# One transfer for each quarter of the routing weights, half of the sorted down matrices kept on chip, and another choice of sorted batches, in a fused mixture-of-experts and attention kernel

## The chip, the cores and the metric

The kernel runs on one core of a Trainium2 chip. The metric is the device time of one execution in microseconds (us). A core has five engines with a queue each, which work in parallel and wait for each other through semaphores: PE (TensorE, matrix products), ACT (ScalarE), DVE (VectorE), POOL (GpSimd) and SP (SyncE). SP computes nothing here: it issues nearly all transfers. A transfer, once issued, is carried by the core's 16 DMA engines. Each queue is strictly in order, so an instruction that waits holds everything behind it.

## The reference

The input is x, 8 batches of 1024 tokens of 128 numbers, all in float32. Three steps follow each other, each added to x:

```
x = x + 0.5 * ffn(layernorm(x))
x = x + causal_attention(layernorm(x))        # one head of 128, rotary positions
x = x + 0.5 * ffn(layernorm(x))               # the same weights again

ffn(h): scores = sigmoid(h @ gate_w.T);  idx = top4(scores + gate_b)
        w = 2.5 * scores[idx] / sum(scores[idx])
        y = sum over 16 experts e of  comb[:, e] * ((silu(h @ gate_e) * (h @ up_e)) @ down_e)
            + the same form with one shared expert, unweighted
```

An expert has 64 inner units; each token uses 4 of the 16 experts.

## The kernel before

**Two ways to compute the ffn.** Tokens are handled in groups of 512 (four tiles of 128), two groups to a batch. Over the two ffn layers there are 32 groups. Twenty are *dense* (class `Group`): all 16 experts are computed for all tokens, two experts (one pair) per step on the 128 partitions, and the product with `comb` zeroes what a token did not choose. Twelve are *sorted* (class `SortedGroup`), in three chunks of two batches (`CHUNKS`: batches 4 and 5 of the first ffn, then 0 and 1, then 2 and 3 of the second). A chunk counts and places its tokens, scatters normalised rows into a DRAM buffer ordered by expert (`scatter`, L1041, indirect transfers from POOL), works through that buffer in ten double blocks of 1024 rows (class `Rows`), writes results to DRAM, and each token gathers its four results back (`gather`, L868, POOL) and adds them (`gathered`, L877, DVE).

**A dense group.** `gate` (L677) and `up` (L683) are 512-wide products per pair; `gate_act` (ACT), `units` (L694, DVE) and `weigh` (L699, DVE, or POOL as a help) make the hidden tile; `down` (L710) sums nine terms per token tile. `weigh` needs the tile `cb`: for each pair, the routing weights of its two experts, spread over 64 partitions each. The weights are turned on PE, stored to a small DRAM tensor `cd` (`store_weights`, L610) and read back with a broadcast over partitions (`load_weights`, L619) in four quarters of two pairs each. The pairs are experts 2n and 2n+1, so each quarter takes two transfers, one per half of the partitions:

```
for h in range(2):
    nc.sync.dma_start(
        out=cb[h * I : (h + 1) * I, :, :],
        in_=self.pairs[h, part * N : (part + 1) * N, :].unsqueeze(0).broadcast_to([I, N, W]),
    )
```

Here I is 64, N is 2 and W is 512. There are `CBP` = 4 quarter tiles in all, so a quarter of the next group can be loaded once both `weigh` of that quarter are done.

**A double block of sorted rows.** `load` (L1112) brings two times 512 rows, `turn` (L1143) transposes them on PE, `up` (L1154) multiplies with a table of gate and up matrices that lies on chip and is addressed by a register, and after the activation and `turn_units`, `down` (L1187) multiplies with the down matrices `wt`, which `load_down` (L1136) fetches from DRAM with eight small transfers of 32 KB, each at an address read from the sorted owners; `wt` has two buffers. Results leave by `store` (L1200).

**The order.** The program is not written in the order in which it is issued. Class `Plan` is a list scheduler at build time: every step has an engine, an estimated duration, a rank (lower first), the steps it follows and the buffers it takes and frees. It writes one fixed order per engine. Rank constants are `UNITS`, `WEIGH`, `ATTEND`, `SORT`, `READY`, `EXPERTS`, `HELP`, from 0 to 5000; `PATIENCE` says how long ACT puts off a step that needs another function table. The framework gives SP's transfers eight completion semaphores in turn, so a transfer waits for the one issued eight before it.

Of the kernel before, what the change touches and what calls it, by code (L numbers as in the profile page):

```python
# [43 lines left out]
class Plan:  # L44
# [6 lines left out]
    PATIENCE = 2.0  # L51
    RATE, LAND = 0.23, 1.9

    def __init__(self, begin):
        self.steps = []
        self.places = {}
        self.lines = {}
        self.held = {}
        self.free_at = dict.fromkeys(self.ENGINES, begin)
        self.transfers = begin  # L60
        self.port = begin
        self.table = None
# [9 lines left out]
    def add(self, engine, work, rank, emit, after=(), take=(), free=(), table=None, moves=0,  # L72
            port=False):
        s = Step(engine, work, rank, emit, take, free, table, moves, port)
        for a in after:
            if a.engine is None:
                s.ready = max(s.ready, a.end)
            else:
                a.next.append(s)
                s.left += 1  # L80
        self.steps.append(s)
        return s
# [58 lines left out]
    def run(self):  # L141
# [12 lines left out]
        while todo:  # L154
# [30 lines left out]
            self.free_at[e] = end = t + work  # L185
            if s.port:
                self.port = end
            if s.moves:
                self.transfers = max(end + 0.5, self.transfers) + s.moves / self.RATE
                end = self.transfers + self.LAND  # L190
# [11 lines left out]
def kernel(  # L202
# [30 lines left out]
    CHUNKS = ((0, (4, 5)), (1, (0, 1)), (1, (2, 3)))  # L233
# [28 lines left out]
    for name, n, shape in (  # L262
        ("x", 9, [P, GT, D]),
        ("xn", 3, [P, GT, D]),
        ("xnc", CB * NG + 1, [P, GT, D]),
        ("hT", 3, [P, W]),
        ("hTs", 2, [P, W]),
        ("hTa", 1, [P, W]),
        ("lt", 2, [P, P]),
        ("sc", 3, [P, GT, E]),  # L270
        ("bi", 3, [P, GT, E + TOPK]),
        ("m8", 3, [P, GT, 8]),
        ("rp", 3, [P, GT, E + TOPK]),
        ("sel", 3, [P, GT, E]),
        ("comb", 3, [P, E, GT]),
        ("cT", 2, [P, P]),
        ("cb", CBP, [P, NP // CBP, W]),
        ("sg", 4, [P, W]),
        ("sh", 2, [P, W]),
        ("hid", NP + 2, [P, W]),  # L280
        ("q", 1, [P, S]),
        ("k", 1, [P, S]),
        ("v", 1, [P, NT, D]),
        ("pr", 2, [P, S]),
        ("prT", 2, [P, NT, P]),
        ("chosen", 1, [P, CT, E]),
        ("combc", 1, [P, CT, E]),
        ("at", 1, [P, CT, E]),
        ("top", 1, [P, CT, 8]),
        ("eq", 1, [P, GT, TOPK, E]),  # L290
        ("row", 4, [P, GT, D]),
        ("got", 4, [P, TOPK + 1, D]),
        ("wt", 2, [P, GT, D]),
        ("un", 2, [P, W]),
        ("hs", 2, [P, W]),
    ):
        plan.pool(name, n)
        buffers[name] = [sbuf(shape, f"{name}{m}") for m in range(n)]
# [93 lines left out]
    nc.sync.dma_start(out=wd, in_=w_down.rearrange("(n p) d -> p n d", p=P))  # L392
# [6 lines left out]
    table = sbuf([P, E * D], "table")  # L399
    cs = sbuf([P, 2, S], "cs")  # L400
# [105 lines left out]
    class Group:  # L506
# [101 lines left out]
        def store_weights(self):  # L608
# [4 lines left out]
            self.pairs = cd.rearrange("(n h) s -> h n s", h=2)  # L613

        def load_weights(self, part):
            N = NP // CBP
            cb = buf("cb", (self.id, part))
            for h in range(2):
                nc.sync.dma_start(  # L619
                    out=cb[h * I : (h + 1) * I, :, :],  # L620
                    in_=self.pairs[h, part * N : (part + 1) * N, :].unsqueeze(0).broadcast_to([I, N, W]),
                )

        def spread_steps(self, rank, after, shared, turned):
# [9 lines left out]
            for m in range(CBP):  # L634
                loads.append(
                    sp(
                        2.0 / CBP, rank + 0.01 * m, lambda m=m: self.load_weights(m),
# [91 lines left out]
        def expert_steps(self, p, last, hT, turned, weights, shared):  # L729
# [31 lines left out]
            for part, tiles in enumerate(self.parts):  # L761
# [3 lines left out]
                for k, s in enumerate([*ready, shared]):  # L765
                    steps.append(
                        pe(
                            0.89 * share, rank - 0.5 + 0.1 * part,
# [36 lines left out]
    class SortedGroup(Group):  # L805
# [57 lines left out]
        def fetch(self, j):  # L863
            nc.sync.dma_start(out=buf("got", (self.id, j))[:, TOPK, :], in_=self.kept[:, j, :])
# [10 lines left out]
        def gathered(self, j, k):  # L875
            got = buf("got", (self.id, j))
            nc.vector.scalar_tensor_tensor(  # L877
                got[:, TOPK, :], got[:, k, :], self.chunk.weight[:, self.n * GT + j, k : k + 1],
                got[:, TOPK, :], ALU.mult, ALU.add,
            )  # L880

        def store_sorted(self, j):
            t = self.g * GT + j
            to = in_tiles(out, self.b, slice(t, t + 1)) if self.layer else self.kept[:, j : j + 1, :]
            nc.sync.dma_start(out=to, in_=buf("got", (self.id, j))[:, TOPK : TOPK + 1, :])

        def gather_steps(self, rank, after):
            ends = []
            for j in range(GT):
                a = (self.id, j)  # L890
                r = rank + 0.02 * j
                before = [
                    sp(
                        0.5, r, lambda j=j: self.fetch(j), after=[*after, self.away],
                        take=[("got", a, 1)], moves=0.064,
                    )
                ]
                for k in range(TOPK):
                    got = [
                        pool(  # L900
                            1.27, r, lambda j=j, k=k: self.gather(j, k),
                            after=before if k == 0 else [*after, first], moves=0.064,
                        )
                    ]
                    first = got[0] if k == 0 else first
                    before = [
                        dve(
                            0.36, r, lambda j=j, k=k: self.gathered(j, k), after=[*got, *before],
                            port=True,
                        )  # L910
                    ]
                ends.append(
                    sp(
                        0.5, r, lambda j=j: self.store_sorted(j), after=before, free=[("got", a)],
                        moves=0.064,
                    )
                )
            return ends

    class Chunk:  # L920
# [126 lines left out]
        def steps(self, rank, later, begins, cleared):  # L1047
# [52 lines left out]
            for m, gr in enumerate(self.groups):  # L1100
                gr.ends = gr.gather_steps((later if self.layer == 0 else SORT + 1500 + 10 * n) + 3 + m * 0.1, [*done, *w])

    class Rows:
# [22 lines left out]
        def load_down(self):  # L1126
            w = buf("wt", self.id)
            for h in range(2):
                q = 2 * self.i + h
                _, rows = nc.values_load_multi_w_load_instructions(  # L1130
                    self.chunk.owner[0:1, NS + q * GT : NS + (q + 1) * GT],
                    engines=[mybir.EngineType.SP], min_val=0, max_val=(E - 1) * I,
                    skip_runtime_bounds_check_because="the owner is held below the number of experts",
                )
                for j, row in enumerate(rows):
                    nc.sync.dma_start(  # L1136
                        out=w[h * I : (h + 1) * I, j, :], in_=w_down[bass.ds(row, I), :]
                    )
# [44 lines left out]
        def down(self):  # L1183
            for j in range(GT):
                for h in range(2):
# [3 lines left out]
                        buf("wt", self.id)[rows, j, :],  # L1189
# [15 lines left out]
        def steps(self, rank, owner, scattered, in_front):  # L1205
# [3 lines left out]
                moves=0.25,  # L1209
# [286 lines left out]
    def load_table(n):  # L1496
# [5 lines left out]

    have_table = chain(
        sp, READY, [given(100.0)], *[(0.5, lambda n=n: load_table(n)) for n in range(2)], moves=1.0
# [16 lines left out]
    cleared = [given(40.0)]  # L1521
    rows_free = []
    for m in range(2):
        cleared = [
            chain(
                sp, SORT + 900, cleared,
                *[(0.5, lambda m=m, part=part: clear(10 * m + part, 20)) for part in range(10)],
                moves=5.2,
# [129 lines left out]
```

## Time and profile before

| | |
|---|---|
| median of 3 runs | 925.82 us (921.67 to 927.11) |
| the profiled execution: its own time | 927.32 us |
| its span, first to last instruction | 925.5 us |
| mean granted TensorE clock | 0.987 |
| PE, DVE, POOL, ACT busy | 882.7, 689.1, 568.5, 555.3 us |
| bytes moved | 139.52 MB in 173694 packets |
| transfers `cb<-cd` | 160 of 256 KB |
| transfers `wt<-in_w_down` | 240 of 32 KB |

Busy time is the union of an engine's instructions. PE's matrix products are pipelined, and a float32 product shows as two instructions. A group's row reads: line, engine, operation, output and inputs by name, count, busy time, mean duration in ns, then the idle time before it and what ended it. "issue" stands for time in which the engine waited for nothing that the profile shows. "SPq" rows are the time in which SP's queue was issuing. The DMA row of the page is the mean busy share of all 16 DMA engines; it doesn't tell one engine from another. In the list of queues, q1 holds what SP issues, q0 the indirect transfers of POOL.

### The profile page before, as it was taken

To read this page: it belongs to the slowest core of one execution; us is meant where nothing else is said; L and a number is where in the kernel's file an instruction comes from. 1 tells how busy PE (TensorE), PEld (TensorE's weight loads), DVE (VectorE), ACT (ScalarE), POOL (GpSimd) and SP (SyncE) were. 2 spreads that over 40 slices of the span, in tenths; PEclk is the share of its full clock that TensorE was granted. 3 is DMA by queue.
4 is the path that set the end of the run, shared out by engine and by line. 5 is a ranking of instruction groups with operands and counts; after the bars stand their busy time and mean duration, and the time that the engine had idled before them with its cause. 6 is when DMAs were issued, how large, how long until landed. Compare 5 with 4: busy or idle time off the path is not lost.

```text
span 925.5 us, 17703 instructions
## 1 busy us (share of the span) xinstructions
PE 882.7 (95%) x5364; PEld 628.9 (68%) x5364; DVE 689.1 (74%) x2194; ACT 555.3 (60%) x1065; POOL 568.5 (61%) x597
## 2 busy tenths in 40 slices
PE   8899999989999999999899999999998989999998
PEld 5547576558587767778677676667576967666665
DVE  5767888848887776877577898687887646687875
ACT  6566644887875566776467567777657535334321
POOL 3442378887446788547475768887865672177560
PEclk9998999999999999999999999999999989999999
DMA  7979661144576844575566543142567567666671
GB/s 218 237 189 246 165 169 37 35 118 127 139 188 173 223 128 125 157 187 141 161 164 153 158 114 116 39 117 68 153 153 191 147 199 202 174 175 170 156 180 35
DMA packets 173694, 139.52 MB, mean 151 GB/s; under 512 B 17760, under 2 KB 144288, under 8 KB 173472
## 3 DMA queue, kind: packets, MB, share of 16 engines
q1 hardware_dynamic: 160032, 111.95, 46.0%
q0 software_dynamic: 12288, 25.19, 9.7%
q10 hardware_dynamic: 1280, 1.26, 0.4%
q8 instruction: 43, 0.70, 0.3%
q14 instruction: 51, 0.42, 0.1%
HBM read 90.49 MB, written 47.84 MB: 149 GB/s over the span
## 4 chain that ended last, share of the span: by engine, by line
PE 58%; POOL 19%; issue 7%; DMA 5%; ACT 4%; DVE 4%; SPq 1%; ACTq 0%; POOLq 0%; DVEq 0%
PE psum L710 13%; POOL rows L1041 12%; PE psum L677 9%; PE psum L683 9%; PE psum L1154 5%; DMA row<-rows 3%; PE psum L1434 3%; PE psum L1143 3%; PE psum L650 3%; PE psum L1187 2%; PE psum L1393 2%; POOL got L868 2%; PE psum L496 2%; PE psum L1421 1%; POOL mv_f L471 1%
## 5 line engine op out<-in xcount | busy, mean ns | idle before, releaser
L868 POOL DMA_INDIRECT got<-results,place x192 | 189.2, 985 | 99.5 <-issue 45.0
L1041 POOL DMA_INDIRECT rows<-xnc,place x192 | 194.8, 1014 | 75.5 <-issue 54.4
L710 PEld LDWEIGHTS psum<-wd,hid 128*128 128x128 f32 x1280 | 159.9, 194 | 33.1 <-issue 20.3
L710 PE MATMUL psum<-wd,hid 128*128 128x128 f32 x1280 | 168.3, 279 | 4.8 <-issue 2.5
L690 ACT ACTIVATE sg<-psum 128x512 f32<-128x512 f32 x160 | 94.5, 597 | 121.6 <-PE psum L677 98.9
L677 PE MATMUL psum<-hT,wg 128*128 128x512 f32 x320 | 164.7, 596 | 1.7 <-ACT sg L690 1.6
L683 PE MATMUL psum<-hT,wu 128*128 128x512 f32 x320 | 163.4, 592 | 0.0
L694 DVE TENSOR_TENSOR hid<-psum,sg 128x512 f32<-128x512 f32 x160 | 109.3, 688 | 56.5 <-PE psum L683 46.9
L683 PEld LDWEIGHTS psum<-hT,wu 128*128 128x128 f32 x320 | 60.8, 190 | 76.5 <-issue 71.5
L699 DVE TENSOR_TENSOR hid<-hid,cb 128x512 f32<-128x512 f32 x132 | 100.7, 770 | 3.0
L1434 PEld LDWEIGHTS psum<-v,prT 128*128 128x128 f32 x576 | 70.1, 192 | 14.3 <-issue 7.8
L1434 PE MATMUL psum<-v,prT 128*128 128x128 f32 x576 | 74.1, 278 | 1.8 <-DVE prT L1425 1.3
L1393 PE MATMUL psum<-k,q 128*128 128x512 f32 (+2 forms) x192 | 71.0, 504 | 3.9 <-POOL k L1310 3.5
L677 PEld LDWEIGHTS psum<-hT,wg 128*128 128x128 f32 x320 | 51.9, 191 | 26.3 <-issue 20.0
L877 DVE SCALAR_TENSOR_TENSOR got<-got,wk 128x128 f32<-128x128 f32 x192 | 65.2, 358 | 3.8 <-DMA got<-results,place 2.1
L1306 POOL TENSOR_TENSOR sg<-sg,cs 128x512 f32<-128x512 f32 x32 | 40.3, 1281 | 44.7 <-ACT sg L1296 44.5
L1154 PE MATMUL psum<-table,hTs 128*128 x480 | 64.3, 282 | 0.1
L1154 PEld LDWEIGHTS psum<-table,hTs 128*128 128x128 f32 x480 | 59.3, 195 | 5.6 <-issue 2.2
L455 DVE BATCH_NORM_STATS2 st<-x 128x6 f32<-128x128 f32 x192 | 53.2, 277 | 11.2 <-DMA x<-in_x 5.1
L1407 ACT ACTIVATE pr<-psum,top 128x128 f32<-128x128 f32 (+3 forms) x64 | 47.5, 745 | 12.1 <-DVE top L1402 11.7
L1425 ACT COPY prT<-psum 128x512 f32<-128x512 f32 (+3 forms) x85 | 37.2, 477 | 27.0 <-PE psum L1421 25.1
L1393 PEld LDWEIGHTS psum<-k,q 128*128 128x128 f32 x192 | 32.8, 196 | 26.3 <-issue 16.1
(148 smaller groups left out, 1515.5 us busy)
## 6 DMA issues: line engine op xcount, KB each, us to landing
cb<-cd SPq DMA_DIRECT2D x160, 256.0 KB
row<-rows SPq DMA_DIRECT2D x60, 256.0 KB
results<-row SPq DMA_DIRECT2D x60, 256.0 KB
rows<-sums SPq DMA_DIRECT2D x20, 512.0 KB
wt<-in_w_down SPq DMA_DIRECT2D x240, 32.0 KB
x<-in_x SPq DMA_DIRECT2D x16, 256.0 KB
kept<-x SPq DMA_DIRECT2D x12, 256.0 KB
rows<-xnc,place POOLq DMA_INDIRECT x192
```

Source lines behind the costliest of these rows:

```text
L677: nc.tensor.matmul(pair_of(("gu", self.id, k))[0], wg[:, k * P : (k + 1) * P], self.hT(), start=True, stop=True,)
L683: nc.tensor.matmul(pair_of(("gu", self.id, k))[1], wu[:, k * P : (k + 1) * P], self.hT(), start=True, stop=True,)
L690: nc.scalar.activation(buf("sg", a), pair_of(a)[0], AF.Silu)
L694: nc.vector.tensor_tensor(buf("hid", a), pair_of(a)[1], buf("sg", a), ALU.mult)
L699: engine.tensor_tensor(hid, hid, cb, ALU.mult)
L710: nc.tensor.matmul(y[:, cols], units[:, cols], wsd if k == NP else wd[:, k, :], start=(self.terms[part] == 1 and j == tiles[0]), stop=(sel ...
L868: nc.gpsimd.indirect_dma_start(out=buf("got", (self.id, j))[:, k, :], out_offset=None, in_=self.chunk.results, in_offset=bass.IndirectOffs ...
L877: nc.vector.scalar_tensor_tensor(got[:, TOPK, :], got[:, k, :], self.chunk.weight[:, self.n * GT + j, k : k + 1], got[:, TOPK, :], ALU.mul ...
L1041: nc.gpsimd.indirect_dma_start(out=row_views[self.n % 2][t * TOPK + k], out_offset=bass.IndirectOffsetOnAxis(ap=self.place[:, t, k : k + 1 ...
L1154: nc.tensor.matmul(p[:, cols], buf("hTs", (self.id, h))[:, cols], table[:, bass.ds(self.at[h][j], D)], start=True, stop=True,)
L1393: nc.tensor.matmul(s[:, c:e], q[:, i * P : self.width], k[:, c:e], start=True, stop=True)
L1434: nc.tensor.matmul(o, buf("prT", self.id)[:, j, :], buf("v", self.b)[:, j, :], start=(j == 0), stop=(j == i),)
```

## The change

- `load_weights`: the pairs are now experts n and n+8 (the gate, up and down matrices are laid out to match by the host and by two loads of `wd`), so that a quarter of the weights of one half is contiguous in DRAM, and one transfer fills all 128 partitions of a quarter. Its step is costed 0.6 instead of 0.5.
- `load_down` fetches only the second half of a double block (four transfers instead of eight). For the first half, `down` reads a tile `low` on chip, loaded once, which holds all 16 down matrices in partitions 0 to 63, at an address in a register; partitions 64 to 127 of `low` are four `wt` buffers.
- `gather_steps`: one fetch and one store per sorted group instead of four of each. The sum is made in a tile of the pool `x` (which has nine), and `got` loses its fifth row.
- `un` and `hs` get one buffer each instead of two.
- `CHUNKS`: batches 5 and 6 are sorted in the first ffn, not 4 and 5.
- The planner: `PATIENCE` 3.5 instead of 2.0; SP's transfers are modelled with eight lanes (`LANES`), several pieces where a step issues several; `down` of a dense group is ranked behind that group's own gates (+0.5 instead of -0.5); the gathers of the second ffn are ranked `SORT + 500` instead of `SORT + 1500`, ahead of `READY`; the clearing of the second row buffer may start at 160 instead of following the first.

```diff
-    PATIENCE = 2.0
+    PATIENCE = 3.5
+    LANES = 8
...
+            if s.moves and e == "SP":
+                end = t
+                for _ in range(s.pieces):
+                    end = max(end, self.lanes[self.lane]) + work / s.pieces
+                    self.transfers = max(end + 0.5, self.transfers) + s.moves / s.pieces / self.RATE
+                    self.lanes[self.lane] = self.transfers + self.LAND
+                    self.lane = (self.lane + 1) % self.LANES
...
-    CHUNKS = ((0, (4, 5)), (1, (0, 1)), (1, (2, 3)))
+    CHUNKS = ((0, (5, 6)), (1, (0, 1)), (1, (2, 3)))
...
-        ("got", 4, [P, TOPK + 1, D]),
-        ("wt", 2, [P, GT, D]),
-        ("un", 2, [P, W]),
-        ("hs", 2, [P, W]),
+        ("got", 4, [P, TOPK, D]),
+        ("un", 1, [P, W]),
+        ("hs", 1, [P, W]),
...
-            self.pairs = cd.rearrange("(n h) s -> h n s", h=2)
+            self.pairs = cd.rearrange("(h n) s -> h (n s)", h=2)
...
-            for h in range(2):
-                nc.sync.dma_start(
-                    out=cb[h * I : (h + 1) * I, :, :],
-                    in_=self.pairs[h, part * N : (part + 1) * N, :].unsqueeze(0).broadcast_to([I, N, W]),
-                )
+            nc.sync.dma_start(
+                out=cb.rearrange("p n s -> p (n s)"),
+                in_=self.pairs[:, part * N * W : (part + 1) * N * W].unsqueeze(1).broadcast_to(
+                    [2, I, N * W]
+                ),
+            )
...
-                            0.89 * share, rank - 0.5 + 0.1 * part,
+                            0.89 * share, rank + 0.5 + 0.1 * part,
...
-        def fetch(self, j):
-            nc.sync.dma_start(out=buf("got", (self.id, j))[:, TOPK, :], in_=self.kept[:, j, :])
+        def fetch(self):
+            nc.sync.dma_start(out=x_of(self.b, self.g), in_=self.kept)
...
-                gr.ends = gr.gather_steps((later if self.layer == 0 else SORT + 1500 + 10 * n) + 3 + m * 0.1, [*done, *w])
+                gr.ends = gr.gather_steps((later if self.layer == 0 else SORT + 500 + 10 * n) + 3 + m * 0.1, [*done, *w])
...
-            for h in range(2):
-                q = 2 * self.i + h
+            q = 2 * self.i + 1
...
+                nc.sync.dma_start(
+                    out=buf("wt", self.id)[I:, j, :], in_=w_down[bass.ds(row, I), :]
+                )
...
-                        buf("wt", self.id)[rows, j, :],
+                        buf("wt", self.id)[rows, j, :] if h else low[rows, bass.ds(self.at[0][j], D)],
```

## The prediction

> **What bounds the kernel now.** I read the page's busy times first, then the rows over time, the queues, PE's waits, and SP's own instructions.
>
> ```profile
> PE 882.7 (95%) x5364; PEld 628.9 (68%) x5364; DVE 689.1 (74%) x2194; ACT 555.3 (60%) x1065; POOL 568.5 (61%) x597
> ...
> PEclk9998999999999999999999999999999989999999
> DMA  7979661144576844575566543142567567666671
> ```
>
> PE is at work in 882.7 of 925.5 us; only 43 us of it are idle. The change neither adds nor drops a matrix product, so a gain can only come out of those 43 us and the few slices in which the granted clock dips. The DMA row has room: its mean over 16 engines is 56.5% (the sum of the shares below). That is what a change that makes transfers worse would eat.
>
> ```profile
> q1 hardware_dynamic: 160032, 111.95, 46.0%
> q0 software_dynamic: 12288, 25.19, 9.7%
> ...
> cb<-cd SPq DMA_DIRECT2D x160, 256.0 KB
> ...
> wt<-in_w_down SPq DMA_DIRECT2D x240, 32.0 KB
> ```
>
> SP's queue q1 carries 112 MB, of which the routing weights (`cb<-cd`) are 42 MB: the largest stream. Next, what PE waits for:
>
> ```profile
> PE psum L1143 <- DMA row<-rows: 10.5, 8, 3.3
> PE psum L1421 <- ACT pr L1407: 4.7, 5, 1.4
> PE psum L496 <- DVE q L1299: 3.5, 2, 3.0
> ```
>
> The largest wait, 10.5 us in 8 pieces, is for blocks of sorted rows. Two slices around such waits also show the clock down:
>
> ```profile
> 450.00:475.00 25.00, 22.29 (x142) 16.21 (x140) 15.61 (x45) 15.50 (x31) 12.45 (x14) 0.93 0.70 189
> ...
> 750.00:775.00 25.00, 21.77 (x133) 17.17 (x134) 11.71 (x36) 11.82 (x23) 16.03 (x17) 0.86 0.73 199
> ...
> 850.00:875.00 25.00, 25.00 (x124) 15.76 (x123) 20.67 (x56) 9.63 (x16) 13.63 (x15) 1.00 0.66 161
> ```
>
> (columns: window, length, busy us and count of PE, PEld, DVE, ACT, POOL, then clock, DMA share, GB/s). Lost clock: (1 - 0.93) and (1 - 0.86) times 25, 1.75 + 3.5 = 5.25 us. In the last row PE is busy throughout: the dense tail. Why rows come late is seen on SP:
>
> ```profile
> L1136 SPq DMA_DIRECT2D wt<-in_w_down x240: 427/469/1696, 133.4 to 786.9; - x120
> ...
> L619 SPq DMA_DIRECT2D cb<-cd x160: 573/605/3438, 25.9 to 899.4; - x160
> ```
>
> (min/median/max ns of one issue, first and last start). The eight `wt` issues of a double block stand in one queue with its row loads; in the timeline one such eight takes 5.5 to 7.0 us.
>
> **The change, part by part.** The sums are made against the profiled execution, 927.3 us (span 925.5 and 1.8 around it), which lies 1.5 above the median of 925.8.
>
> *Half of the down matrices from chip.* 120 issues of 0.54 us (0.469 and two register rows of 37 and 29 ns) leave SP: 65 us by the medians, and 80 to 105 by the 5.5 to 7.0 us of an eight. They are not on PE's path themselves; what they release is the row loads behind them. Of the 10.5 us I take 9 as gone and of the 5.25 us of clock 4. The loads of `low` (0.5 MB, once, near 100 us) lie beside other work. PE gets 120 more products with a register address: the chain of waits shows eight such pairs (L1154 x16) at 1.78 to 1.98 us, against 1.79 for L710 x16, so 0 to 0.02 us each, 0 to 2.8 us; I take 1, because most of these pieces show 1.79.
>
> *One fetch and one store per sorted group, one `un` and `hs`.* SP loses 72 issues of 0.43 to 0.50 us. The sum moves into an `x` tile, which four groups of the first chunk hold at once; the loads of other batches stand behind these fetches in SP's queue. Cost on PE's path between -1 (reloads wait less) and +5 (one late batch, like the 5.7 us wait for `row<-rows` in the chain); I take 0. With single `un` and `hs`, a wait of `turn_units` would have the other double block's products queued behind it; the order puts those between, so 0, and up to 0.8 us per block if not (the largest wait of L1178).
>
> *Batches 5 and 6 first.* Batch 4's attention no longer waits for gathered rows: the L1421 wait of 1.1 us at 521 us goes, and something like it may return one batch later. I take -1.5, with bounds -2 and 0.
>
> *Order.* `down` behind the gates, gathers ranked ahead, `PATIENCE`: ACT has 90 table loads in both orders, and the first 60 us of PE's order are almost the same. The clearing of the second buffer moves behind 160 us; where it was (75 to 100, DMA share 1.04) PE was 24.95 of 25 us busy, so nothing is to be won. Two of SP's queue positions matter: the weights of the second group still stand behind ten clearing transfers.
>
> So far -9 - 4 - 1.5 + 1 = -13.5 us.
>
> *One transfer for a quarter: the part that decides.* By the issue row alone it is a gain: 80 issues of 0.605 us fewer, 48 us of SP. But compare how the source is walked. Before, its outermost dimension is the broadcast over I = 64 partitions, `[64, 2, 512]`, and so is the target's. Now the source is `[2, 64, 1024]`: outermost 2, the two halves; the target has 128. No transfer of the trace of before has an outermost dimension under 64, so no row here prices that. The Trainium skill does. In "DMA: Bandwidth & Descriptors", section "Why a DMA increments its semaphore by 16 and not by 1", it says that the number of DMA engines a transfer runs on is the largest up to 16 that divides the outermost dimension (not 1) of *both* sides. Before: 64 and 64, so 16 engines. Now: 2 and 128, so **two engines**, and always the lowest ones. The same page's "Rules for kernel authors" pulls the other way: it tells one to replace two transfers to disjoint partition halves by one over 128 partitions, since both share the same engines. The change follows the second rule and runs into the first.
>
> The price by the row (16 engines): the trace's packet records show the 2 KB packets of q1 at 126 ns mean; 160 x 128 / 16 x 0.126 = 161 us per engine over the whole run, much of it hidden, and the sum stays at -13.5. By the rule: a quarter is 128 packets of 4 KB, 64 on each of two engines. A 4 KB packet is between the 2 KB ones (86 ns at the quiet start, 121 median later) and the 8 KB ones of the rope load (314): 162 to 185 ns by straight lines; POOL's own 4 KB packets show 187 median, 224 mean. I take 175. A quarter then takes 64 x 0.175 = 11.2 us, a group 45, all twenty 80 x 11.2 = 896 us, on those two engines. They also carry their sixteenth of everything else: 0.460 x 925.5 - 161 + 0.097 x 925.5 + 7 (the small queues) - 14 (half of `wt`, 7680 packets of 30 ns) = 348 us. Together 1244 us: **the two engines become the bound**. To that, the start before the first weights (25.9 us, some 17 of them already used by other loads) adds 9, and the end, the last quarter's `weigh`, `down` and store, 10: 1263. What hides part of it now, the room in the DMA row, does not help, since it is on the other fourteen. The -13.5 us of PE lie beside it and count nothing. Check by pace: the dense tail runs a group in 23 us (513 PE instructions in the four windows from 800 to 900, about 120 per group); at 45 us and more its five groups alone add 110 us. Every row load that SP issues after a quarter has its share in the same two rings and lands 11 us later per quarter in front of it. I take **1260 us**; its own range is 1150 (162 ns, packed without gaps, and 20 less of other traffic) to 1480 (224 ns gives 1147 + 348; rows late).
>
> **The rivals.**
> *A, two engines (forecast), 1260.* For: the outermost sizes, which can be read in the code, and a rule stated for exactly them. Against: no row here shows it.
> *B, sixteen engines all the same: faster, 912.* If the rule doesn't hold for such a source, what remains is a relieved SP: 927.3 - 13.5 = 913.8 in the profile, 912 as a median. For: the 10.5 us of row waits and the two clock dips sit where SP issues without pause. It decides as soon as a quarter lands in 3 us or so.
> *C, sixteen engines, but gates first starve on DVE: 938.* With `down` behind, eight gate pairs run back to back at 1.72 us (L1286 x4 in the chain), while DVE needs 0.688 + 0.770, and 0.358 for a gathered row, 1.82 us: 0.8 us per group, and about 1.3 when a routing chain falls in. 20 x 1.3 = 26 us, 913.8 + 26 - 1.5 = 938. From 0.7 us per group it eats the gain, from 1.2 it makes the kernel over 1% slower. Against: DVE is only 74% busy and three pairs are in flight.
>
> **How the numbers follow.** A 0.72, B 0.20, C 0.08. About 1% is what a measurement of this kernel tells from no change. Faster: B, less the 0.03 in which its gain stays under 9 us, 0.17. Within 1%: those 0.03 and half of C, 0.07. Slower: A and the other half of C, 0.76. The predicted time is that of A. As A leaves out more than 2 in 10, the range reaches over C to B: 905 to 1450, leaving some of each end out.
>
> **What would show it.** A: the page lists `cb<-cd` x80 at 512 KB; PE falls to about 70% busy, with its clock often down; the mean DMA share *falls* to about 37% (2 x 896 + 16 x 348 engine-us over 16 x 1260), though transfers hold everything up; the largest waits are `hid` at `weigh` (L720) for `cb<-cd`, and `row<-rows`. B: PE above 96%, the L1159 wait for rows under 3 us, no clock dip after 450. C: waits of `wg`/`wu` products for `hid`/`sg` at the top of PE's list. The forecast is wrong if a quarter lands within about 5 us of its issue; the size is wrong if a 4 KB packet takes far from 175 ns.

## The result and the profile after

The changed kernel takes **1303.99 us** (median of 4 runs, 1300.91 to 1304.76) where the kernel before takes 926.19 (921.67 to 927.11) on the same chip: a ratio of **1.409** (95% interval 1.4035 to 1.4138). The forecast was 1260. The profiled execution took 1300.91 us by itself, its span is 1299.1, and the mean granted TensorE clock is 0.865.

First the page of the changed kernel: busy times, the rows of the clock and of the DMA engines, the two large queues, the shares of the chain that ended last, and the transfers of the routing weights.

```profile
PE 962.3 (74%) x5364; PEld 685.6 (53%) x5364; DVE 683.1 (53%) x2187; ACT 561.0 (43%) x1072; POOL 562.8 (43%) x597
...
PEclk9798879996878879978898898999798777978876
DMA  6251142521211144433453443212335343522211
...
q1 hardware_dynamic: 131552, 108.52, 26.1%
q0 software_dynamic: 12288, 25.19, 7.0%
...
DMA cb<-cd 33%; DMA row<-rows 13%; PE psum L731 5%; DMA results<-row 4%; PE psum L698 4%; PE psum L704 3%; DMA kept<-x 3%; PE psum L1170 3%; DMA cd<-cT 2%; PE psum L1159 2%; PE psum L1409 2%; POOL rows L1059 2%; DMA x<-kept 2%; PE psum L1450 2%; SPq L638 1%
...
cb<-cd SPq DMA_DIRECT2D x80, 512.0 KB
```

PE is at work for 74% of the span and its clock dips everywhere, not in two slices. The DMA row has *fallen*: 26.1 + 7.0 + 0.7 for the small queues is 33.8%, against 56.5% before. Read alone, it says that transfers have room. The line of the chain says the opposite: a third of the chain is the landing of `cb<-cd`. Both are true if a few of the sixteen engines carry that stream, so that the mean over sixteen hides how full those few are. The 80 transfers of 512 KB show that the change did what it says.

The list of waits (us in total, times, longest):

```profile
DVE hid L720 <- DMA cb<-cd: 184.7, 28, 11.1
...
PE psum L1159 <- DMA row<-rows: 129.6, 14, 22.1
...
POOL hid L720 <- DMA cb<-cd: 102.5, 11, 28.7
```

`weigh` (L720) waits 287 us for routing weights on DVE and POOL together. In the kernel before the one such wait of note was a single one of POOL's:

```profile
POOL hid L699 <- DMA cb<-cd: 15.8, 1, 15.8
```

The wait of the row transposes went from 10.5 to 129.6 us. The chain in order of time (start, length, what) shows the weights at the start and at the end:

```profile
28.71 40.60 DMA cb<-cd
...
82.92 20.21 DMA cb<-cd
103.12 23.74 DMA cd<-cT
127.57 18.26 DMA cb<-cd
...
1148.22 87.08 DMA cb<-cd x3
1237.01 19.67 DMA cb<-cd
1257.79 29.55 DMA cb<-cd
```

The first group's weights take 40.6 us; a dense group of the old tail took 23 us in all. By the packet records its four quarters land one after the other, at 38.6, 48.6, 58.8 and 68.8 us. At 103 us even the small store of a group's weights (`cd<-cT`, 32 KB) needs 23.7 us, and only then can the group's own quarters start: the packet records show an earlier group's quarters under way through all of that time, from 86 to 126 us. The tail is the weights and little else: the last quarter lands at 1287.3. By stage (window, length, busy us and count of PE, PEld, DVE, ACT, POOL, clock, DMA share, GB/s):

```profile
1200.00:1299.00 99.00, 62.19 (x234) 43.00 (x234) 35.24 (x73) 10.14 (x17) 17.12 (x18) 0.76 0.20 71
```

The row of the old tail showed PE busy in 25.00 of 25 us, at clock 1.00 and a DMA share of 0.66. Here it is busy in 62 of 99, at 0.76, with a DMA share of 0.20. Last, SP's own instructions (ns of one issue: min/median/max):

```profile
L638 SPq DMA_DIRECT2D cb<-cd x80: 484/632/18359, 26.5 to 1257.8; - x80
```

The median issue is about what it was (605), and there are half as many. But one of them now holds SP for 18 us, where the longest of them before was 3.4, and it is not alone: 33 of SP's 432 issues take over 8 us, and all of them together 850 us, against 396 for the 702 issues of the kernel before. What such an issue waits for is not shown.

The packet records of the trace (start, duration, bytes and queue of each packet, but not its engine) settle the size. SP's 10240 packets of 4 KB, all of them routing weights, take 159 ns in the median and 163 in the mean. At least one is under way in 854 us of the span, and in 445 us none is; in 139 of these no packet of any queue is under way.

The records also show on how many engines a transfer runs. In the kernel before, SP's 702 transfers leave, besides their data, exactly 702 x 16 = 11232 packets of 4 bytes. Call these closing packets, and read them as one for each engine that carried the transfer. In the changed kernel the 432 transfers leave 5792 = 352 x 16 + 80 x 2: **two for each transfer of weights**. The packets under way bear the reading out: in 752 of the 854 us exactly two packets of weights are under way at once. SP has issued three quarters by 28.7 us, and still, until the first has landed at 38.6, there are two at once for 9.7 of 10.7 us: the quarters share the same two engines.

The trace also shows how other transfers are held up. Three of them stand behind the first group's weights: a load of 512 packets, a store of 64 and a clearing of 1024. Of these 448, 56 and 896 start by 64.1 us, fourteen sixteenths each time. The other two sixteenths start only after 67 us, and the weights end at 68.8. So a transfer on sixteen engines waits with two sixteenths of itself behind the weights.

### The profile page after: what moved, and what is told of

Its sections match the earlier page's. It is cut to its first block, busy times and chain, and to the rows that moved or that the text cites. A ratio compares the mean times of both kernels' runs of the same rounds, so it can differ in the third digit from the quotient of the medians.

```text
span 1299.1 us, 17112 instructions
## 1 busy us (share of the span) xinstructions
PE 962.3 (74%) x5364; PEld 685.6 (53%) x5364; DVE 683.1 (53%) x2187; ACT 561.0 (43%) x1072; POOL 562.8 (43%) x597
## 3 DMA queue, kind: packets, MB, share of 16 engines
q1 hardware_dynamic: 131552, 108.52, 26.1%
## 4 chain that ended last, share of the span: by engine, by line
DMA 58%; PE 28%; DVE 4%; POOL 3%; SPq 3%; issue 2%; ACT 2%; ACTq 0%; DVEq 0%; POOLq 0%
DMA cb<-cd 33%; DMA row<-rows 13%; PE psum L731 5%; DMA results<-row 4%; PE psum L698 4%; PE psum L704 3%; DMA kept<-x 3%; PE psum L1170 3%; DMA cd<-cT 2%; PE psum L1159 2%; PE psum L1409 2%; POOL rows L1059 2%; DMA x<-kept 2%; PE psum L1450 2%; SPq L638 1%
## 5 line engine op out<-in xcount | busy, mean ns | idle before, releaser
L731 PE MATMUL psum<-wd,hid 128*128 128x128 f32 x1280 | 200.5, 315 | 74.8 <-DVE hid L720 49.2
L731 PEld LDWEIGHTS psum<-wd,hid 128*128 128x128 f32 x1280 | 188.3, 228 | 92.8 <-DVE hid L720 48.3
L1059 POOL DMA_INDIRECT rows<-xnc,place x192 | 190.7, 993 | 64.1 <-issue 53.8
L704 PE MATMUL psum<-hT,wu 128*128 128x512 f32 x320 | 174.4, 628 | 28.6 <-DVE hid L715 27.9
L720 DVE TENSOR_TENSOR hid<-hid,cb 128x512 f32<-128x512 f32 x132 | 96.3, 737 | 187.3 <-DMA cb<-cd 184.7
L698 PE MATMUL psum<-hT,wg 128*128 128x512 f32 x320 | 172.9, 623 | 0.9 <-ACT sg L711 0.9
L1159 PE MATMUL psum<-ident,row 128*128 128x128 f32 x240 | 44.4, 322 | 143.2 <-DMA row<-rows 129.6
L1159 PEld LDWEIGHTS psum<-ident,row 128*128 128x128 f32 x240 | 32.9, 165 | 154.7 <-DMA row<-rows 100.3
L720 POOL TENSOR_TENSOR hid<-hid,cb 128x512 f32<-128x512 f32 x28 | 36.8, 1327 | 133.2 <-DMA cb<-cd 102.5
L898 DVE SCALAR_TENSOR_TENSOR x<-got,wk,x 128x128 f32<-128x128 f32 x192 | 69.1, 375 | 20.7 <-DMA got<-results,place 11.2
L698 PEld LDWEIGHTS psum<-hT,wg 128*128 128x128 f32 x320 | 56.5, 200 | 38.8 <-issue 34.6
L1163 ACT COPY hTs<-psum 128x512 f32<-128x512 f32 x49 | 28.8, 589 | 111.0 <-PE psum L1159 110.6
```

What stands on the lines that cost most here:

```text
L698: nc.tensor.matmul(pair_of(("gu", self.id, k))[0], wg[:, k * P : (k + 1) * P], self.hT(), start=True, stop=True,)
L704: nc.tensor.matmul(pair_of(("gu", self.id, k))[1], wu[:, k * P : (k + 1) * P], self.hT(), start=True, stop=True,)
L720: engine.tensor_tensor(hid, hid, cb, ALU.mult)
L731: nc.tensor.matmul(y[:, cols], units[:, cols], wsd if k == NP else wd[:, k, :], start=(self.terms[part] == 1 and j == tiles[0]), stop=(sel ...
L1059: nc.gpsimd.indirect_dma_start(out=row_views[self.n % 2][t * TOPK + k], out_offset=bass.IndirectOffsetOnAxis(ap=self.place[:, t, k : k + 1 ...
L1159: nc.tensor.transpose(pt[:, j, :], buf("row", (self.id, h))[:, j, :], ident)
```

## The experiments

Two kinds of chip turn up below. On some the kernel before took 924 to 926 us, on the others 1176 to 1180, the same program; so each time is compared only with that of the kernel before on the same chip, as a ratio. The names "quicker" and "slower kind" stand for these two levels; whether the chip itself or something beside the program makes them is not known. The second kind is looked at under the last heading. The theory: the outermost dimension of 2 puts each transfer on two engines, and that is the whole loss. The rivals: a single transfer is late as such; the loss comes from another part of the change.

### The two transfers back (slower kind of chip, then quicker kind)

```diff
-            nc.sync.dma_start(
-                out=cb.rearrange("p n s -> p (n s)"),
-                in_=self.pairs[:, part * N * W : (part + 1) * N * W].unsqueeze(1).broadcast_to(
-                    [2, I, N * W]
-                ),
-            )
+            for h in range(2):
+                nc.sync.dma_start(
+                    out=cb[h * I : (h + 1) * I, :, :].rearrange("p n s -> p (n s)"),
+                    in_=self.pairs[h, part * N * W : (part + 1) * N * W].unsqueeze(0).broadcast_to(
+                        [I, N * W]
+                    ),
+                )
```

> The changed kernel, but each quarter of the weights goes in two transfers again, one per half of the partitions, each with the broadcast over 64 partitions as the source's outermost dimension. Pairs n and n+8, packets of 4 KB, the planner's costs and the whole order stay as changed. Two-engine theory: both sides have 64 outermost, so 16 engines, and the time falls to what the prediction gave its rival B, 905 to 920 us. Rival 'large packets': it is the 4 KB packets or the re-pairing that cost, then it stays within 5% of 1304 us. Rival 'order': the new order, the x tiles or gates-first cost, then it also stays above 1200 us.

1155.0 us on the slower kind of chip, where the kernel before took 1176.0: a ratio of 0.981 (0.977 to 0.985). The time missed its range with the chip; the ratio is what was expected. On the quicker kind:

> The changed kernel with each quarter in two transfers again (one for each half of the partitions, 4 KB packets). The first run of this edit was on a chip where the kernel before took 1176 us instead of 926. Theory (the engine count of the single transfer is the whole loss): where the kernel before takes about 926 us this takes 900 to 920, a ratio of 0.97 to 0.995, and the mean DMA share comes back to 42 to 48%; where the kernel before takes about 1176, a ratio of 0.977 to 0.985 again. Rival (on a quick chip the pairing, the sorted batches or the reads on chip cost something of their own): a ratio over 1.01.

**907.89 us against 923.99, a ratio of 0.982** (0.977 to 0.986). Everything else of the change is still in this kernel, so the way in which the single transfer is written alone turns a gain of 1.8% into a loss of 41%. Its page:

```profile
PE 877.9 (97%) x5364; PEld 626.7 (69%) x5364; DVE 689.4 (76%) x2187; ACT 559.7 (62%) x1072; POOL 574.8 (63%) x597
...
q1 hardware_dynamic: 133952, 108.53, 45.0%
q0 software_dynamic: 12288, 25.19, 10.4%
```

PE is at 97%, and the mean DMA share is back at 56.4%. PE's list of waits has no wait for rows left:

```profile
PE psum L1410 <- POOL k L1327: 4.5, 4, 1.7
PE psum L1028 <- DVE ows L1006: 3.7, 1, 3.7
PE psum L732 <- DVE hid L721: 3.3, 2, 2.8
```

### Two engines and four engines, with two transfers (slower kind of chip)

The broadcast over 64 partitions of the two transfers is written as 2 x 32 and as 4 x 16; bytes, packets and targets stay.

```diff
-                    in_=self.pairs[h, part * N * W : (part + 1) * N * W].unsqueeze(0).broadcast_to(
-                        [I, N * W]
+                    in_=self.pairs[h, part * N * W : (part + 1) * N * W].unsqueeze(0).unsqueeze(0).broadcast_to(
+                        [2, I // 2, N * W]
```

> As e1_halves (two transfers per quarter, one per half), but the broadcast over 64 partitions is written as 2 x 32, both with stride zero: the same packets from the same addresses to the same places, only the source's outermost dimension is 2. Two-engine theory: two engines again, near 1300 us (1250 to 1350), though each transfer is only 256 KB. Rival 'one large transfer' (512 KB waits for all of itself, two of 256 KB don't): the time of e1_halves.

> As e2_k2 with the broadcast written as 4 x 16. Two-engine theory, as a rule of the outermost size: four engines, 160 x 16 x 0.163 = 417 us on each for the weights and some 340 for the rest, 760 in all, which no longer bounds the whole run, but a group's weights take 8 x 16 x 0.163 = 21 us, about as long as PE needs for it in the dense tail: 915 to 980 us. Without that rule: the time of e1_halves.

With 2 outermost 1396.4 us, a ratio of 1.186 (1.180 to 1.192); with 4 outermost 1182.6, 1.005 (1.002 to 1.009); with 64 it was 0.981. The 1396 is over the 1300 that was expected, on a chip where everything is slower; the order of the three is as expected. Nothing but the shape in which a zero-step dimension is written differs between the three. So the outermost size decides, with the number of transfers held at two. The closing packets of 4 bytes count the engines, and the weight packets under way at once agree:

| outermost size | transfers per quarter | closing packets per transfer | weights under way, us | most frequent number at once |
|---|---|---|---|---|
| 2 (the changed kernel) | 1 | 2 | 854 | 2, in 752 us |
| 2 | 2 | 2 | 892 | 2, in 763 us |
| 4 | 2 | 4 | 507 | 4, in 355 us |
| 64 (the section above, slower kind) | 2 | 16 | 216 | 16, in 50 us |

The version with four was run once more on another chip:

> The changed kernel with each quarter in two transfers whose outermost dimension is 4 (four engines each, packets of 4 KB). On the chip where the kernel before took 1176 us it was 2.4% slower than with sixteen engines. Theory: four engines carry 418 us of the weights and some 340 of the rest each, 758 us, so it hides as in the run with two quarters: 905 to 960. Rival (any transfer on fewer than sixteen engines is late in proportion, one seventh of the loss of two engines): 906 plus 57, about 963 or more.

1181.2 us, a ratio of 1.002 (0.998 to 1.006): four engines cost about 2% against sixteen on this kind of chip (2.4% in the first run). The expectation gave times for the quicker kind, where the theory allowed up to 6% over sixteen engines (960 against 906) and the rival asked for more. On the slower kind the whole loss of two engines is only 0.205, and a seventh of it is 0.029; 0.021 to 0.024 is too near to that to tell the two apart. What stands is that four engines are not free, and cost far less than two.

### One part alone, on the order of before (slower kind of chip)

The kernel before, with the pairing and the single transfer and nothing else of the change.

```diff
-            self.pairs = cd.rearrange("(n h) s -> h n s", h=2)
+            self.pairs = cd.rearrange("(h n) s -> h (n s)", h=2)
...
+            nc.sync.dma_start(
+                out=cb.rearrange("p n s -> p (n s)"),
+                in_=self.pairs[:, part * N * W : (part + 1) * N * W].unsqueeze(1).broadcast_to(
+                    [2, I, N * W]
+                ),
+            )
```

> The kernel before with this part of the change alone: experts paired n and n+8, one transfer per quarter with the source's outermost dimension 2; its planner, its order and all else as before. Two-engine theory: 836 us of weights and about 360 of other packets on two engines, and gaps as in the changed kernel: 1250 to 1350 us. Rival 'order': 915 to 935 us, since nothing of the order is new.

1475.3 us, a ratio of 1.253 (1.246 to 1.260), 299 us more than the kernel before on that chip. The time missed its range with the chip; as a loss, 299 us lies a little under the 324 to 424 that the range meant against 926. The part alone carries the loss. It is 79 us longer than the changed kernel with two engines (1396.4, same chip). A packet takes the same (median 159 ns in both) and weights are under way for about as long (847 and 892 us), but in 624 us, against 502, none is under way. What of the other parts shortens that was not taken apart.

### The pairing alone (quicker kind of chip)

The kernel before, pairs n and n + 8, still two transfers per quarter; packets of 4 KB.

```diff
-                    in_=self.pairs[h, part * N : (part + 1) * N, :].unsqueeze(0).broadcast_to([I, N, W]),
+                    in_=self.pairs[h, part * N * W : (part + 1) * N * W].unsqueeze(0).broadcast_to(
+                        [I, N * W]
+                    ),
```

> The kernel before with the pairing alone: experts paired n with n + 8, so that a packet of the weights is 4 KB and not 2 KB, still two transfers per quarter, and the order, the reads of down matrices and the chunks as before. Theory (pairing costs and brings nothing beside other work, since each of sixteen engines is at work under half of the time): a ratio of 0.99 to 1.01. Rival (the pairing carries a gain or a loss of its own, through the different rows that a gate group covers): under 0.99 or over 1.01.

927.6 us against 924.0, a ratio of 1.005 (1.001 to 1.008): within what was expected, if anything a little slower. Its wait for rows stands where it stood before (10.5):

```profile
PE psum L1149 <- DMA row<-rows: 10.9, 8, 2.9
```

So the 16 us that the two-transfer version gains come, on the order of before, from neither the pairing nor the packet size.

### One transfer, but 64 outermost (quicker kind of chip)

Expert n goes to the even partitions and n + 8 to the odd ones, so that the broadcast stays outermost in one transfer. The down matrices come in that order as one more input, `w_pair`, laid out by the host as the gate and up matrices are.

```diff
-                in_=self.pairs[:, part * N * W : (part + 1) * N * W].unsqueeze(1).broadcast_to(
-                    [2, I, N * W]
+                in_=self.pairs[:, part * N * W : (part + 1) * N * W].unsqueeze(0).broadcast_to(
+                    [I, 2, N * W]
...
-        return w.reshape(2, E // 2, I, D).transpose(1, 0, 2, 3).reshape(E * I, D)
+        return w.reshape(2, E // 2, I, D).transpose(1, 2, 0, 3).reshape(E * I, D)
```

> The changed kernel with one transfer per quarter kept, but expert n on the even partitions and n + 8 on the odd ones, so that the outermost dimension of the transfer is 64 and not 2 (the down matrices are given to the kernel in that order in one more input). Theory (two engines are the loss, not the single transfer): all sixteen engines carry it, and the kernel is as quick as with two transfers per quarter or up to 1% quicker, since SP issues 80 fewer: a ratio of 0.97 to 0.99 to the kernel before. Rival (a single transfer of 512 KB is itself late, since its first row comes only with the last packet of the whole quarter): 1.02 to 1.15.

**905.89 us, a ratio of 0.980** (0.976 to 0.985): faster than both kernels of this study, and not to be told from the two transfers (907.89). One transfer of 512 KB is not late as such; two of 256 KB are not better. From its page:

```profile
PE 873.8 (97%) x5364; PEld 625.0 (69%) x5364; DVE 691.6 (76%) x2187; ACT 559.3 (62%) x1072; POOL 574.3 (64%) x597
...
DMA  7672440923544354866476553214242887555550
...
q1 hardware_dynamic: 132656, 108.52, 39.7%
...
cb<-cd SPq DMA_DIRECT2D x80, 512.0 KB
```

The same 80 transfers of 512 KB as in the changed kernel, with PE at 97% instead of 74%. The bytes of q1 are the same too (108.52 MB), but there are 1104 more packets: fourteen more closing packets for each of the 80 transfers, less the sixteen of one load that this version saves. So each now runs on sixteen engines. The list of who waits for them has one entry, POOL's 13.0 us, against 287 us:

```profile
L635 SPq DMA_DIRECT2D cb<-cd x80: 512/555/3299, 25.5 to 872.7; - x80
...
  POOL hid L717: 13.0, 1
```

### A dose: two, then three of four quarters in the single transfer (slower kind of chip, then quicker)

Quarters 1 and 3, and then 1, 2 and 3 (counted from 0), keep the single transfer; the others take the two transfers shown above.

```diff
+            if part in (1, 3):
...
+                return
+            for h in range(2):
...
```

> The changed kernel with the second and fourth quarter of each group in the single transfer (two engines) and the other two in two transfers each (sixteen engines). Theory (the time is what two engines must carry, and it decides only once it is longer than the rest): two quarters of each group are half of the 836 us that the single transfers took on each of the two engines, 418, and with some 340 us of everything else these have 758 us of work, under the 906 of the kernel without single transfers: 905 to 970, the excess over 906 being bursts. Rival (each single transfer costs its lateness, so the loss goes with their number): half of the 398 us between 906 and 1304, so about 1105.

> The changed kernel with three quarters of each group in the single transfer and one in two transfers. Theory (what two engines must carry): 627 us of single transfers plus some 340 us of the rest make 967 us on the two engines, just over the 906, and with the share of gaps that the changed kernel had (1304 against 1176) 1000 to 1100. Rival (loss in proportion to the number of single transfers): about 1205.

1208.1 and 1268.6 us; the times missed their ranges with the chip. The ratios are 1.024 (1.017 to 1.030) and 1.074 (1.067 to 1.081), between 0.981 with none and 1.186 with the two-engine version of all four. The steps, 0.043, 0.050 and 0.112, grow: half the dose brings a fifth of the whole 0.205, three quarters less than half. That is against a loss in proportion, and fits a bound that is crossed. On the quicker kind of chip:

> The changed kernel with three quarters of each group in the single transfer and one in two transfers, once more: the first run of it was on the chip where the kernel before took 1180 us (ratio 1.074 there, 1.024 with two quarters, 0.981 with none). Where the kernel before takes about 926 us: theory (what two engines must carry, 627 us of single transfers and some 340 of the rest, 967, with gaps) 1000 to 1100, a ratio of 1.08 to 1.19; rival (three quarters of the loss of four, 906 plus 299) about 1205, a ratio of 1.30. Where it takes about 1180 again: 1.065 to 1.085, and nothing new is told apart.

1151.9 us against 924.6, a ratio of 1.245 (1.241 to 1.249). **Both expectations missed**: over the 1000 to 1100 of the theory, under the 1205 of the rival. The packet records say why:

| quicker kind of chip | span, us | at least one 4 KB packet of weights under way | none |
|---|---|---|---|
| all four quarters single (the changed kernel) | 1299.1 | 854.0 | 445.1 |
| three quarters single | 1150.2 | 706.0 | 444.2 |
| none single, two transfers | 907.4 | 233.2 | 674.2 |

From three to four the span grows by 148.9 us and the time with weights under way by 148.0, while the rest stays at 444 to 445. So one sum that fits is a sum of *time*: weights under way, and a remainder of some 444 us in which none is. The sum of work that I had used fits as well once its idle time is put right, which makes it no more than an estimate: with 627 us for the single transfers (7680 packets at 163 ns on two engines), 40 for a sixteenth of the other quarter's packets, which I had left out, and 337 for a sixteenth of all else, the two engines work for 1004 us and idle for 146. The changed kernel has 836 + 335 = 1171 of work and 128 idle. The runs do not choose between the two sums. What the expectation had too small in either is the time in which the two engines have nothing to do. On the slower kind the remainder does not stay: it is 502 us with two engines for all four quarters, 564 for three and 652 for two. The wait in the largest line on the quicker kind is the same one at a smaller size:

```profile
DVE hid L729 <- DMA cb<-cd: 114.3, 17, 10.2
```

With none single the sum no longer holds, since PE is the bound there and the stretches lie side by side. An estimate for two quarters by the sum of time: 444 + 427 (half of 854) + 117 (half of 233) = 988 us; it was not run on the quicker kind.

### SP's issues given back (slower kind of chip)

The version with two transfers, each of its 120 reads of a down matrix in two issues of 32 rows: 240 again.

```diff
-                nc.sync.dma_start(
-                    out=buf("wt", self.id)[I:, j, :], in_=w_down[bass.ds(row, I), :]
-                )
+                for m in range(2):
+                    nc.sync.dma_start(
+                        out=buf("wt", self.id)[I + m * 32 : I + (m + 1) * 32, j, :],
+                        in_=w_down[bass.ds(row + m * 32, 32), :],
+                    )
```

> The changed kernel with two transfers per quarter, and each of its 120 reads of a sorted down matrix from DRAM in two issues of 32 rows, so that the sync engine issues 240 of them as in the kernel before. Theory (the gain of 16 us of the two-transfer version over the kernel before is mostly what the sync engine was relieved of, so that sorted rows are no longer late): the waits of the row transposes for their rows come back by 5 us or more and the time rises to 911 to 922. Rival (the gain comes from the new order and from the sorted batches, with the sync engine having time to spare): 905 to 910.

1160.2 us, a ratio of 0.986 (0.979 to 0.993), against 0.981 (0.977 to 0.985) for the same version with 120 issues on another chip. The intervals overlap. The theory's other sign, waits of the row transposes for their rows that come back by 5 us or more, did not appear: PE's list has no such wait, as it has none with 120 issues. On this kind of chip, where all else is later, that is weak evidence against the theory and no more. That SP's relief is what brings the 16 us stays open.

## Why the prediction was right, and where its terms were off

**The deciding step held.** What the Trainium skill says in "DMA: Bandwidth & Descriptors", section "Why a DMA increments its semaphore by 16 and not by 1" (the engine count is the largest up to 16 that divides both outermost sizes) was cited with no row of the trace beside it. The runs now put rows there: 2, 4 and 64 outermost gave 2, 4 and 16 closing packets per transfer, and ratios of 1.186, 1.005 and 0.981 on one chip. The prediction's "always the lowest ones" is shown in part: the quarters share the same two engines, but the records do not name them. All three sizes are powers of two, so no run here tells a common divisor from the smaller of the two sizes. The chip's description had a transfer carried by the core's 16 DMA engines; that holds only where the outermost sizes allow it. The page's other rule, in "Rules for kernel authors", that one transfer over 128 partitions should take the place of two over halves, cost 41% as the change follows it and nothing where 64 stays outermost. The same list has a row that joins the two: an outermost dimension under 16, a leading broadcast for example, confines the whole transfer. That is the row to read first.

**The sum was 1263, with errors against each other.** The packet was taken as 175 ns and takes 163, so the two engines carry 836 us of weights, not 896. Everything else per engine was worked out as 348 us and is 335 by the records, if it is spread evenly. These make the sum too large by 73. The other way, the two engines were given almost no idle time: 9 us at the start and 10 at the end. Measured, 836 + 335 = 1171 us of work stand in a span of 1299, which leaves 128 us idle where the sum has 19; and in 139 us no packet of any queue is under way at all. So the term that was mis-sized most is the gaps, by 109 us. The end alone was well sized: from the landing of the last quarter, 1287.3, to 1299.1 are 11.8 us. Why the order leaves the two engines idle in between was not taken apart. That 1260 came within 4% of 1304 is in part luck: with the right packet and the right traffic the same sum gives 1190. The ends of its own range were loose too: by their terms the low one is 829 + 328 = 1157, not 1150, and the high one 1147 + 348 = 1495, not 1480.

**SP's share.** By the issue row alone the single transfer was a gain of 48 us of SP. SP's issues now take 850 us instead of 396, since some wait long. A median taken where nothing is held up did not carry over to a stream that is.

**What would show it.** `cb<-cd` x80 at 512 KB: yes. PE about 70%: 74. A mean DMA share that falls to about 37%: 33.8. The largest waits `hid` at L720 and `row<-rows`: yes, 184.7 and 129.6 us. The pace of a group, 45 us: 40.6 for the first, and its quarters land about 10 us apart, where 11.2 was worked out and under 5 would have spoken against the forecast.

**The small steps, in the version with two transfers.** They count nothing in the changed kernel, as stated, and can be read where the cover is gone: 907.89 against 923.99 is -16.1 us, where the sum was -13.5. Of the 10.5 us of waits for rows 9 were taken as gone; PE's list has none left. PE's busy time falls by 4.8 us (882.7 to 877.9), where 4 were taken for the clock; the mean clock itself hardly moves (0.987 to 0.988), so how much of the 4.8 is the clock is not shown. The products with a register address, taken at +1 us, cost nothing that shows: the group of `down` has 272 ns as its median before and after, and a mean of 285 for those that read `wt` before, and for those that read `low` now.

**The rivals.** B, sixteen engines after all, was 912 us by the sum; restoring sixteen engines gives 905.9 and 907.9. Its size was right and its premise false. C, gates that starve on DVE, 938, does not occur in either of these versions: the largest entry in PE's list is 4.5 us, for another line, and with two transfers the gates wait 0.9 us for `sg` and the products of `up` 0.7 us for `hid`.

## What to carry to other kernels

Before two transfers are made one, write down the outermost dimension of both sides as the instruction carries it: 2 outermost cost 1.41x here, and the same bytes in the same single transfer with 64 outermost cost nothing. A DMA row that fell, from 56.5 to 33.8%, while waits for a transfer rose was here the sign of a stream confined to few engines; the mean over sixteen hides it, and the number of packets in the queue's line shows it (131552 against 132656 for the same bytes). Where a stream becomes the bound, give the engines that carry it idle time too: here 128 us, where the forecast had 19.

## What was not expected of the hardware

**A 4 KB packet.** Its median is 159 ns on two engines (changed kernel) and on four (slower kind of chip). With two transfers over sixteen it is 265 ns (246 on the slower kind), and in one transfer with 64 outermost 159 again, with a mean of 195. Two streams side by side against one is a reading of this; no run takes it apart.

**The other kind of chip.** The kernel before takes 1176 us there instead of 926. It has no profile there, but the version with two transfers has one on each kind. On the slower kind its list of waits has entries whose releaser the trace ties to no instruction of the core ("remote"):

```profile
ACT prT L1442 <- remote: 72.0, 11, 19.9
...
DVE x L742 <- remote: 40.1, 5, 14.9
```

On the quicker kind none is among the largest. A stretch in the middle of one such wait (same columns as above):

```profile
220.00:233.00 13.00, 0.00 (x0) 0.00 (x0) 1.91 (x5) 0.29 (x1) 6.76 (x8) 0.50 0.12 40
```

PE does nothing for 13 us, DVE and ACT next to nothing, and the DMA share is 0.12; POOL issues indirect transfers for half of it. Stretches of over 2 us between two of their instructions in which PE, DVE and ACT all stand still add up to 111 us of the span; the same version on the quicker kind has none. What holds the engines is not shown. Each comparison was made on one chip, so its direction stands, but the ratios are smaller there: 1.186 there for two engines with two transfers, where the quicker kind shows 1.41 for the changed kernel and its single one.
